# Q, k and v of a graph transformer layer by seven half-sized fp32 block products (Strassen's scheme), and the second group's rows transposed on TensorE

**Chip, cores, metric.** One core of one Trainium2 chip (trn2). The metric is the device time of one execution in microseconds, the median of several.

## The reference, cut to what matters

128 batches of 128 rows of 512 numbers go through two layers. The change touches only the projections of the first.

```python
h = jnp.maximum(_layernorm(x, axis=-1), 0.0)
q, k, v = (proj(Wq, bq), proj(Wk, bk), proj(Wv, bv))     # each: 'bse,fe->bsf', 512 x 512
scores = jnp.einsum('bhqd,bhkd->bhqk', q, k) * SCALE     # 8 heads of 64
attn = jax.nn.softmax(scores * mask, axis=-1)            # mask = 2 * adj
x = x + jnp.einsum('bse,fe->bsf', ctx, Wo) + bo          # ctx = attn @ v
# ... a graph attention layer with one 512 x 512 matrix, softmax over rows, elu
```

## The kernel before

Batches come in groups of four (G = 4). One iteration of the main loop handles scores and context of batch t, the output projection of t - 1 and the second layer of t - 2, and projects a quarter of q and k of the next group, so that TensorE (PE) always has something to do. Everything is fp32. The parts concerned:

```python
def qk_unit(g, n):                        # one of 8 blocks of q, k for a group of 4 batches
    f, is_k = divmod(n, 2)
    ...
    pp = ps1.tile([P, G * S], F32, name="pp", tag="ps1")
    for c in range(C):                    # C = 4 chunks of 128 of the contraction
        nc.tensor.matmul(pp, w[:, c, f * P : (f + 1) * P],
                         hTs[g][:, c].rearrange("p b s -> p (b s)"),     # 512 columns
                         start=(c == 0), stop=(c == C - 1))
    return lambda: nc.scalar.activation(dst, pp, AF.Identity, bias=...)  # eviction
def values(b):                            # v of one batch, 4 matmuls of 512 columns
    pv = rows_matmul(hTs[g][:, :, i, :], wv_sb)
    nc.scalar.copy(vs[b], pv)
def spread0(b): ...                       # mean and 1/std of each row: SBUF -> DRAM
def fetch0(b): ...                        # ... and back, as rows broadcast over partitions
def hidden(b): ...                        # transposed x -> hidden rows, with them
# start (cut): group 0's rows are transposed on TensorE, group 1's go by the DRAM trip
for n in range(2 * C):
    b = G + n // 2
    evict = qk_unit(0, n)
    if n % 2 == 0:
        stats0(b); spread0(b); fetch0(b)
    else:
        load_x0(b + G)
    evict()
    if n > 2 and n % 2:
        hidden(b - 1)
hidden(2 * G - 1)
# main loop (cut), iteration t:
    scores(t); evict = qk_unit(g + 1, 2 * i)
    scores1(t - 2)                        # second layer: one transpose (pb), softmax follows
    evict(); normalise(t); softmax1(t - 2); output0(t - 1); values(t); gather1(t - 2)
    qk_unit(g + 1, 2 * i + 1)(); hidden(ahead)
    attn_T(t); output1(t - 2); context(t)
```

Of the kernel before, what the change touches and what calls it, by code (L numbers as in the profile page):

```python
# [13 lines left out]
P = 128  # L14
# [3 lines left out]
H = 8  # L18
# [5 lines left out]
def kernel(  # L24
# [30 lines left out]
    work = ctx.enter_context(tc.tile_pool(name="work", bufs=2))  # L55
    small = ctx.enter_context(tc.tile_pool(name="small", bufs=6))
    ps1 = ctx.enter_context(tc.tile_pool(name="ps1", bufs=4, space=bass.MemoryType.PSUM))
    ps2 = ctx.enter_context(tc.tile_pool(name="ps2", bufs=2, space=bass.MemoryType.PSUM))

    xs, x0s, adjs, adjTs, hTs = {}, {}, {}, {}, {}  # L60
# [11 lines left out]
    def hT_slot(b):  # L72
        g, i = divmod(b, G)
        if i == 0:
            hTs[g] = grp.tile([P, C, G, S], F32, name="hT", bufs=3)
        return hTs[g][:, :, i, :]

    def load_xT(b):
        nc.sync.dma_start(hT_slot(b), xT[b])  # L79
# [30 lines left out]

    bq_sb = column(bq, "bq")
    bk_sb = column(bk, "bk")
    bv_sb = column(bv, "bv")
    wq_sb = weight(wqT, "wq")
    wk_sb = weight(wkT, "wk")
    for b in range(G, 2 * G):
        load_xT(b)
    wv_sb = weight(wvT, "wv")
# [6 lines left out]
    for b in range(2):  # L125
        load_adj(b)
# [24 lines left out]
    def norm0(b):  # L151
        mv, rstd = st0.pop(b)
        hns[b] = work.tile([P, E], F32, name="hn", tag="h2", bufs=4)
        nc.vector.tensor_scalar(hns[b], x0s.pop(b), mv[:, 0:1], rstd, op0=OP.subtract, op1=OP.mult)
# [18 lines left out]
    def fetch0(b):  # L173
        r = rows0[b]
        rows0[b] = small.tile([P, 2, S], F32, name="mr", bufs=3)
        nc.sync.dma_start(rows0[b].rearrange("p s k -> p (s k)"), r.rearrange("s p -> (s p)").partition_broadcast(P))

    def hidden(b):

        mr = rows0.pop(b)  # L180
        g, i = divmod(b, G)
        h = hTs[g][:, :, i, :]
# [10 lines left out]
    def qk_unit(g, n):  # L193

        f, is_k = divmod(n, 2)
        if n == 0:
            qks[g] = grp.tile([P, C, G * S], F32, name="qT"), grp.tile([P, C, G * S], F32, name="kT")
        w = wk_sb if is_k else wq_sb
        dst = qks[g][is_k][:, f]
        pp = ps1.tile([P, G * S], F32, name="pp", tag="ps1")  # L200
        for c in range(C):
            nc.tensor.matmul(  # L202
                pp, w[:, c, f * P : (f + 1) * P], hTs[g][:, c].rearrange("p b s -> p (b s)"),
                start=(c == 0), stop=(c == C - 1),
            )
        if is_k:
            return lambda: nc.scalar.activation(dst, pp, AF.Identity, bias=bk_sb[:, f : f + 1])  # L207
        return lambda: nc.scalar.activation(dst, pp, AF.Identity, bias=bq_sb[:, f : f + 1], scale=QSCALE)

    def values(b):  # L210
        g, i = divmod(b, G)
        pv = rows_matmul(hTs[g][:, :, i, :], wv_sb)
        vs[b] = work.tile([P, E], F32, name="v")
        nc.scalar.copy(vs[b], pv)  # L214

    def scores(b):
        g, i = divmod(b, G)
        qT, kT = qks[g]
# [7 lines left out]
        at = work.tile([P, H, S], F32, name="at", bufs=3)  # L226
        nc.vector.tensor_tensor(at, sc, adjs[b][:, None, :].to_broadcast([P, H, S]), OP.mult)  # L227
        nmx = small.tile([P, H], F32, name="nmx")
        nc.vector.tensor_reduce(nmx, at, AX.X, OP.max, negate=True)  # L229
        sums = small.tile([P, H], F32, name="sums")  # L230
# [19 lines left out]
    def context(b):  # L250

        pc = ps1.tile([P, C, S], F32, name="pc", tag="ps1")
        for i in range(C):
            for s in range(2):
                head = 2 * i + s
                nc.tensor.matmul(  # L256
                    pc[s * D : (s + 1) * D, i, :], vs[b][:, head * D : (head + 1) * D], ats[b][:, s * C + i, :],
# [5 lines left out]
    def output0(b):  # L263
        po = rows_matmul(cxs[b], wo_sb)
        nc.vector.tensor_tensor(xs[b], po, xs[b], OP.add)
        mv, rstd = row_stats(xs[b])

        h2 = work.tile([P, E], F32, name="h2", bufs=4)
# [24 lines left out]
    def softmax1(b):  # L293
        h2, w, nmx, rstd = l1s[b]
        sums = small.tile([P, 1], F32, name="sums1")
        nc.scalar.activation(w, w, AF.Exp, bias=nmx, accum_out=sums)
        rs = small.tile([P, 1], F32, name="rs1")
# [51 lines left out]


    with tc.manual_schedule():
        nc.scalar.mul(bq_sb, bq_sb, QSCALE)
        for b in range(G):
            stats0(b)
        for b in range(G):
            norm0(b)
            hidden_T(b)
            load_x0(G + b)
        for n in range(2 * C):
            b = G + n // 2  # L360
            evict = qk_unit(0, n)
            if n % 2 == 0:
                stats0(b)
                spread0(b)
                fetch0(b)
            else:
                load_x0(b + G)
            evict()
            if n > 2 and n % 2:
                hidden(b - 1)  # L370
        hidden(2 * G - 1)
        load_x(0)
        load_x(1)
        load_xT(2 * G)
        stats0(2 * G)
        spread0(2 * G)
        stats0(2 * G + 1)
        for t in range(B + 3):
            g, i = divmod(t, G)
            more = (g + 1) * G < B  # L380
            ahead = t + 2 * G
# [3 lines left out]
            if ahead < B:  # L385
                fetch0(ahead)
            if ahead + 4 < B:
                load_x0(ahead + 4)
            if ahead + 1 < B:
                spread0(ahead + 1)  # L390
            if t < B:
                scores(t)
            if more:
                evict = qk_unit(g + 1, 2 * i)
            if t == 1:
                spread_u()
            if 0 <= t - 2 < B:
                scores1(t - 2)
            if more:
                evict()  # L400
            if t < B:
                normalise(t)
            if 0 <= t - 2 < B:
                softmax1(t - 2)
            if 0 <= t - 1 < B:
                output0(t - 1)
            if t < B:
                values(t)
            if 0 <= t - 2 < B:
                gather1(t - 2)  # L410
            if more:
                qk_unit(g + 1, 2 * i + 1)()
            if ahead < B:
                hidden(ahead)
            if ahead + 2 < B:
# [50 lines left out]
```

## Time and profile before

| | before |
|---|---|
| median, lowest to highest of 3 | 2821.45 us, 2820.44 to 2821.62 |
| PE, VectorE (DVE), ScalarE (ACT) busy | 97%, 56%, 39% |
| steady iteration, scores to scores | 21.36 us, of it 10.31 us q, k and v |
| PE without work at the first iteration | 39.3 us |
| scores of batch 2 start | 122.65 us after the start |
| an iteration of the last group | 16.36 us |

How to read it: PE is the bound, so time is what PE does one thing after another. A matmul's busy time runs up to its modelled end, which overlaps the next one; the pace is read from the distance of starts. The prediction below shows the lines.

In the lines, `sc` is the scores, `pa` the transposes of the attention, `pc` the context, `pb` and `pg` the second layer's transpose and its gather. `pm` is a block with 512 columns: with `wo` the output projection, with `w` the second layer's matrix, with `wv` v. `pp` is q and k before the change; `acc_a` to `acc_c` are the products after it, one for each bank of PSUM, the memory that the matmuls write to and that ScalarE and VectorE read. `[39.3 <-DVE hT L184]` means that the engine had been idle for 39.3 us, and what released it. The granted clock is the share of TensorE's full clock that the profile shows as granted.

### The profile page before, as it was taken

How to read it: one execution, taken by the hardware profiler on the slowest of the kernel's cores; microseconds unless marked ns; L12 is line 12 of the kernel's file. 1: busy time of each engine (PE TensorE's matmuls, PEld its weight loads, DVE VectorE, ACT ScalarE, POOL GpSimd, SP SyncE). 2: the span in 40 equal slices, each digit the busy share in tenths (PEclk: the TensorE clock that was granted, in tenths of full speed). 3: DMA queues.
4: the chain of work that ended last, by engine and by line, in shares of the span. 5: the costliest groups of instructions: out<-in, count | busy, mean ns of one | idle time of the engine just before them, and what ended most of it. 6: DMA issues, size and time to landing. Idle time of an engine off the chain costs nothing.

```text
span 2821.7 us, 33182 instructions
## 1 busy us (share of the span) xinstructions
PE 2750.6 (97%) x11424; PEld 1431.5 (51%) x11424; DVE 1581.7 (56%) x3085; ACT 1100.9 (39%) x3336; POOL 415.2 (15%) x647
## 2 busy tenths in 40 slices
PE   4799999999999999999999999999999999999997
PEld 2355555555555555555555555555555555555554
DVE  1555655655555565565565555556556555555545
ACT  1334344334433433433433343343443334434343
POOL 1111111111111111111111111111111111111101
PEclk8999999999999999999999999999999999999999
DMA  5412112112212211211221221221121122122110
GB/s 151 58 61 71 57 57 74 57 57 70 62 57 63 69 57 56 75 57 56 71 61 57 65 67 57 59 73 56 57 72 60 56 67 65 57 61 60 34 38 19
DMA packets 214040, 174.55 MB, mean 62 GB/s; under 512 B 49648, under 2 KB 161776, under 8 KB 213872
## 3 DMA queue, kind: packets, MB, share of 16 engines
q1 hardware_dynamic: 212288, 172.42, 21.3%
q8 instruction: 91, 1.49, 0.4%
q14 instruction: 77, 0.63, 0.1%
q10 hardware_dynamic: 1584, 0.01, 0.0%
HBM read 138.68 MB, written 33.68 MB: 61 GB/s over the span
## 4 chain that ended last, share of the span: by engine, by line
PE 94%; DMA 3%; DVE 1%; ACT 1%; SPq 0%; issue 0%; POOL 0%; ACTq 0%; DVEq 0%
PE pm L142 46%; PE pp L202 31%; PE sc L225 5%; PE pc L256 5%; PE pg L307 4%; PE pa L245 4%; DMA rows<-mv 2%; ACT at L232 1%; PE pb L285 0%; DMA mr<-rows 0%; DMA c<-in_bo 0%; DVE nmx L229 0%; DVE at L227 0%; DVE junk L337 0%; DMA x<-in_x 0%; SPq L79 0%
## 5 line engine op out<-in xcount | busy, mean ns | idle before, releaser
L232 ACT ACTIVATE at<-at,nmx 128x128 f32<-128x128 f32 x1024 | 395.8, 388 | 426.9 <-DVE nmx L229 426.9
L202 PE MATMUL pp<-hT,wq 128*128 128x512 f32 x1024 | 474.9, 606 | 40.0 <-DVE hT L184 39.3
L135 POOL TENSOR_SCALAR mv<-mv 128x1 f32<-128x1 f32 x256 | 135.8, 530 | 2303.4 <-DVE mv L132 2303.2
L142 PE MATMUL pm<-w,gT 128*128 128x512 f32 x1024 | 463.1, 595 | 1.5 <-ACT gT L309 1.5
L142 PE MATMUL pm<-wv,hT 128*128 128x512 f32 x1024 | 460.4, 592 | 2.9 <-ACT u_src L347 2.9
L142 PE MATMUL pm<-wo,cxT 128*128 128x512 f32 x1024 | 460.8, 593 | 0.5 <-ACT cxT L261 0.5
L202 PE MATMUL pp<-hT,wk 128*128 128x512 f32 x1024 | 460.6, 592 | 0.0
L317 DVE SCALAR_TENSOR_TENSOR x<-pm,x 128x512 f32<-128x512 f32 x128 | 88.5, 691 | 641.9 <-ACT ez L316 641.9
L142 PEld LDWEIGHTS pm<-wv,hT 128*128 128x128 f32 x1024 | 194.5, 190 | 248.2 <-issue 244.4
L202 PEld LDWEIGHTS pp<-hT,wq 128*128 128x128 f32 x1024 | 184.9, 190 | 241.4 <-issue 186.0
L142 PEld LDWEIGHTS pm<-wo,cxT 128*128 128x128 f32 x1024 | 184.8, 190 | 220.0 <-issue 219.3
L288 DVE TENSOR_TENSOR w<-w,neg 128x128 f32<-128x128 f32 x128 | 37.4, 292 | 441.5 <-ACT w L287 441.5
L142 PEld LDWEIGHTS pm<-w,gT 128*128 128x128 f32 x1024 | 185.3, 191 | 187.1 <-issue 184.7
L202 PEld LDWEIGHTS pp<-hT,wk 128*128 128x128 f32 x1024 | 185.2, 190 | 186.5 <-issue 186.5
L214 ACT COPY v<-pm 128x512 f32<-128x512 f32 x128 | 74.9, 585 | 434.4 <-PE pm L142 434.3
L207 ACT ACTIVATE kT<-pp,bk 128x512 f32<-128x512 f32 x128 | 88.1, 688 | 357.6 <-PE pp L202 357.6
L136 POOL TENSOR_TENSOR mv<-mv,mhalf 128x1 f32<-128x1 f32 x256 | 200.0, 781 | 21.4
L316 ACT ACTIVATE ez<-pm 128x512 f32<-128x512 f32 x128 | 76.5, 598 | 316.2 <-PE pm L142 316.2
L130 DVE BATCH_NORM_STATS2 st<-x 128x6 f32<-128x512 f32 x256 | 176.7, 690 | 25.8 <-DMA x<-in_x 21.2
L232 ACT ACTIVATION_READ_ACCUMULATOR at<-at,nmx 128x1 f32 x1024 | 191.1, 187 | 0.0
L307 PEld LDWEIGHTS pg<-w,h 128*128 128x128 f32 x1024 | 134.8, 193 | 73.0 <-issue 68.7
L227 DVE TENSOR_TENSOR at<-sc,adj 128x1024 f32<-128x1024 f32 x128 | 156.7, 1224 | 6.1 <-PE sc L225 3.7
(59 smaller groups left out, 2763.7 us busy)
## 6 DMA issues: line engine op xcount, KB each, us to landing
x<-in_x SPq DMA_DIRECT2D x256, 256.0 KB, 3.8
out<-x SPq DMA_DIRECT2D x128, 256.0 KB, 2.1
hT<-in_xT SPq DMA_DIRECT2D x124, 256.0 KB, 3.3
mr<-rows SPq DMA_DIRECT2D x124, 128.0 KB, 3.6
adj<-in_adj SPq DMA_DIRECT2D x128, 64.0 KB, 2.8
adjT<-in_adjT SPq DMA_DIRECT2D x128, 64.0 KB, 3.0
rows<-mv SPq DMA_DIRECT2D x124, 1.0 KB, 9.3
wq<-in_wqT SPq DMA_DIRECT2D x1, 1024.0 KB, 7.1
```

The source lines that it names most:

```text
L130: nc.vector.bn_stats(st, src)
L135: nc.gpsimd.tensor_scalar_add(rstd, rstd, EPS)
L136: nc.gpsimd.tensor_tensor(rstd, rstd, mhalf, OP.pow)
L142: nc.tensor.matmul(pm, lhsT[:, c, :], w[:, c, :], start=(c == 0), stop=(c == C - 1))
L202: nc.tensor.matmul(pp, w[:, c, f * P : (f + 1) * P], hTs[g][:, c].rearrange("p b s -> p (b s)"), start=(c == 0), stop=(c == C - 1),)
L225: nc.tensor.matmul(sc[:, s * C + i, :], qT[r, i, cols], kT[r, i, cols], start=True, stop=True)
L227: nc.vector.tensor_tensor(at, sc, adjs[b][:, None, :].to_broadcast([P, H, S]), OP.mult)
L232: nc.scalar.activation(at[:, j, :], at[:, j, :], AF.Exp, bias=nmx[:, j : j + 1], accum_out=sums[:, j : j + 1])
L245: nc.tensor.transpose(pa[:, j, :], at[:, j, :], ident)
L256: nc.tensor.matmul(pc[s * D : (s + 1) * D, i, :], vs[b][:, head * D : (head + 1) * D], ats[b][:, s * C + i, :], start=True, stop=True,)
L307: nc.tensor.matmul(pg[:, c, :], h2[:, c * P : (c + 1) * P], w, start=True, stop=True)
L317: nc.vector.scalar_tensor_tensor(xs[b], pw, 0.0, xs[b], op0=OP.max, op1=OP.add)
```

## The change

The intent is to do less arithmetic on the engine that is the bound. The hidden rows of a group (512 x 512) and each weight (512 x 512) are cut into quarters of 256; q, k and v are each had from seven products of quarters instead of eight, at the price of sums: of weight quarters once, of hidden quarters once a group, and of products when they leave PSUM. Three PSUM banks (a, b, c) collect the products; "a" goes on accumulating after its value so far was read. The second part concerns the start: the second group's rows are normalised and transposed on TensorE, like the first's, instead of by the round trip of their statistics through DRAM.

The diff, cut to its core (`# ...` marks cuts, the other comments are added here):

```diff
-    ps1 = ctx.enter_context(tc.tile_pool(name="ps1", bufs=4, space=bass.MemoryType.PSUM))
-    ps2 = ctx.enter_context(tc.tile_pool(name="ps2", bufs=2, space=bass.MemoryType.PSUM))
+    ps1 = ctx.enter_context(tc.tile_pool(name="ps1", bufs=6, space=bass.MemoryType.PSUM))
+    ps2 = ctx.enter_context(tc.tile_pool(name="ps2", bufs=1, space=bass.MemoryType.PSUM))
# ... work pool bufs 2 -> 1, hT a tile of 7 quarters, weights loaded as quarters
+    def weight_sums(w):                       # once for each of q, k, v
+        nc.vector.tensor_tensor(w[:, 4], w[:, 1], w[:, 0], OP.subtract)
+        nc.vector.tensor_tensor(w[:, 5], w[:, 3], w[:, 4], OP.subtract)
+        nc.vector.tensor_tensor(w[:, 1], w[:, 3], w[:, 1], OP.subtract)
+        nc.vector.tensor_tensor(w[:, 6], w[:, 2], w[:, 5], OP.subtract)
+    PRODUCTS = [(0, 0, "a"), (1, 2, "b"), (5, 5, "a"), (6, 1, "c"), (4, 4, "a"), (2, 3, "a"), (3, 6, "c")]
+    def hidden_sums(g):                       # once a group
+        h = hTs[g]
+        nc.vector.tensor_tensor(h[:, 4], h[:, 2], h[:, 3], OP.add)
+        nc.vector.tensor_tensor(h[:, 5], h[:, 4], h[:, 0], OP.subtract)
+        nc.vector.tensor_tensor(h[:, 6], h[:, 0], h[:, 2], OP.subtract)
+        nc.vector.tensor_tensor(h[:, 2], h[:, 1], h[:, 5], OP.subtract)
-    def qk_unit(g, n):
# ...
+    def product(g, which, n):
+        ha, wb, bank = PRODUCTS[n]
# ...
+        for m in range(2):
+            ms = slice(m * P, (m + 1) * P)
+            for c in range(2):
+                lhsT, rhs = (h[:, c, ms], w[:, wb, c, :]) if which == "v" else (w[:, wb, c, ms], h[:, c, :])
+                nc.tensor.matmul(                                   # 256 columns
+                    acc[:, m, :], lhsT, rhs, start=fresh and m == 0 and c == 0, stop=c == 1, skip_group_check=True
+                )
# ... first(): ScalarE copies bank a out; add(): VectorE adds bank b or c to what is there
+    SEQ = ["q0", "q1", "q2", "q3", "q4", "k0", "q5", "k1", "q6", "k2", "k3", "k4", "v0", "k5", "v1", "k6"]
+    SEQ += ["v2", "v3", "v4", "v5", "v6"]
+    TICKS = [SEQ[0:5], SEQ[5:10], SEQ[10:15], SEQ[15:21]]
     with tc.manual_schedule():
# ... start: all 21 products of group 0, between them for each batch of group 1:
-                spread0(b)
-                fetch0(b)
+                    norm0(b)
+            if b < 2 * G and step == 3:
+                hidden_T(b)
+        stats0(2 * G)
# ... spread0(2 * G), stats0(2 * G + 1)
+        hidden_sums(1)
+        stats0(2 * G + 2)
# ... main loop:
+            if 0 <= t - 2 < B:
+                scores1(t - 2)                # now ahead of scores(t)
+                softmax1(t - 2)
             if t < B:
                 scores(t)
+                mask(t)                       # with the scale of q in it
+            done = unit(0)
# ... exps, hidden or hidden_sums, normalise, output0(t - 1), products 1 to 3
#     around hidden1 and gather1, attn_T(t), product 4, output1, product 5, context(t)
```

More of the change, by code (lines that the diff above doesn't have):

```diff
@@ L54 @@
     grp = ctx.enter_context(tc.tile_pool(name="grp", bufs=2))
-    work = ctx.enter_context(tc.tile_pool(name="work", bufs=2))
+    work = ctx.enter_context(tc.tile_pool(name="work", bufs=1))
     small = ctx.enter_context(tc.tile_pool(name="small", bufs=6))
-    ps1 = ctx.enter_context(tc.tile_pool(name="ps1", bufs=4, space=bass.MemoryType.PSUM))
-    ps2 = ctx.enter_context(tc.tile_pool(name="ps2", bufs=2, space=bass.MemoryType.PSUM))
-    xs, x0s, adjs, adjTs, hTs = {}, {}, {}, {}, {}
+    ps1 = ctx.enter_context(tc.tile_pool(name="ps1", bufs=6, space=bass.MemoryType.PSUM))
+    ps2 = ctx.enter_context(tc.tile_pool(name="ps2", bufs=1, space=bass.MemoryType.PSUM))
+    xs, x0s, adjs, adjTs, hTs, hslots = {}, {}, {}, {}, {}, {}
     def load_x(b):
@@ L74, in hT_slot @@
         if i == 0:
-            hTs[g] = grp.tile([P, C, G, S], F32, name="hT", bufs=3)
-        return hTs[g][:, :, i, :]
+            hTs[g] = grp.tile([P, 7, 2, 2 * S], F32, name="hT")
+        half, w = divmod(i, 2)
+        return hTs[g][:, 2 * half : 2 * half + 2].rearrange("p q c k -> p (q c) k")[:, :, w * S : (w + 1) * S]
     def load_xT(b):
-        nc.sync.dma_start(hT_slot(b), xT[b])
+        hslots[b] = hT_slot(b)
+        nc.sync.dma_start(hslots[b], xT[b])
     def load_adj(b):
@@ L109, in row, with quarters @@
         return b
+    def quarters(src, name):
+        w = const.tile([P, 7, 2, E // 2], F32, name=name)
+        nc.sync.dma_start(w[:, 0:4], src)
+        return w
     bq_sb = column(bq, "bq")
@@ L113 @@
     bv_sb = column(bv, "bv")
-    wq_sb = weight(wqT, "wq")
-    wk_sb = weight(wkT, "wk")
+    wq_sb = quarters(wqT, "wq")
+    wk_sb = quarters(wkT, "wk")
     for b in range(G, 2 * G):
-        load_xT(b)
-    wv_sb = weight(wvT, "wv")
+        load_x0(b)
+    wv_sb = quarters(wvT, "wv")
+    for b in range(2):
+        load_adj(b)
+        load_x(b)
     wo_sb = weight(woT, "wo")
@@ L123 @@
     ut_sb = row(a1, E, "u_dst")
-    for b in range(2):
-        load_adj(b)
+    def weight_sums(w):
[3 more added lines that the diff above has]
+        nc.vector.tensor_tensor(w[:, 6], w[:, 2], w[:, 5], OP.subtract)
     def row_stats(src):
@@ L152, in norm0 @@
         mv, rstd = st0.pop(b)
-        hns[b] = work.tile([P, E], F32, name="hn", tag="h2", bufs=4)
+        hns[b] = work.tile([P, E], F32, name="hn", tag="h2", bufs=3)
         nc.vector.tensor_scalar(hns[b], x0s.pop(b), mv[:, 0:1], rstd, op0=OP.subtract, op1=OP.mult)
@@ L174, in fetch0 @@
         r = rows0[b]
-        rows0[b] = small.tile([P, 2, S], F32, name="mr", bufs=3)
+        rows0[b] = small.tile([P, 2, S], F32, name="mr", bufs=4)
         nc.sync.dma_start(rows0[b].rearrange("p s k -> p (s k)"), r.rearrange("s p -> (s p)").partition_broadcast(P))
@@ L180, in hidden @@
         mr = rows0.pop(b)
-        g, i = divmod(b, G)
-        h = hTs[g][:, :, i, :]
+        h = hslots.pop(b)
         nc.vector.tensor_tensor(h, h, mr[:, 0:1, :].to_broadcast([P, C, S]), OP.subtract)
@@ L191, in shift @@
         nc.vector.tensor_tensor(xs[b], xs[b], c_sb, OP.add)
-    def qk_unit(g, n):
-        f, is_k = divmod(n, 2)
-        if n == 0:
-            qks[g] = grp.tile([P, C, G * S], F32, name="qT"), grp.tile([P, C, G * S], F32, name="kT")
-        w = wk_sb if is_k else wq_sb
-        dst = qks[g][is_k][:, f]
-        pp = ps1.tile([P, G * S], F32, name="pp", tag="ps1")
-        for c in range(C):
-            nc.tensor.matmul(
-                pp, w[:, c, f * P : (f + 1) * P], hTs[g][:, c].rearrange("p b s -> p (b s)"),
-                start=(c == 0), stop=(c == C - 1),
-            )
-        if is_k:
-            return lambda: nc.scalar.activation(dst, pp, AF.Identity, bias=bk_sb[:, f : f + 1])
-        return lambda: nc.scalar.activation(dst, pp, AF.Identity, bias=bq_sb[:, f : f + 1], scale=QSCALE)
@@ L210, in values @@
-    def values(b):
-        g, i = divmod(b, G)
-        pv = rows_matmul(hTs[g][:, :, i, :], wv_sb)
-        vs[b] = work.tile([P, E], F32, name="v")
-        nc.scalar.copy(vs[b], pv)
+    PRODUCTS = [(0, 0, "a"), (1, 2, "b"), (5, 5, "a"), (6, 1, "c"), (4, 4, "a"), (2, 3, "a"), (3, 6, "c")]
[5 more added lines that the diff above has]
+        nc.vector.tensor_tensor(h[:, 2], h[:, 1], h[:, 5], OP.subtract)
@@ new lines, with dst, first, add @@
+    accs = {}
+    def product(g, which, n):
+        if n == 0:
+            if which == "v":
+                vs[g] = grp.tile([P, G, E], F32, name="v")
+            else:
+                qks[g, which] = grp.tile([P, C, G * S], F32, name=which + "T")
+        w = {"q": wq_sb, "k": wk_sb, "v": wv_sb}[which]
+        ha, wb, bank = PRODUCTS[n]
+        fresh = (which, bank) not in accs
+        if fresh:
+            accs[which, bank] = ps1.tile([P, 2, 2 * S], F32, name="acc_" + bank, tag="ps1")
+        acc = accs[which, bank]
+        h = hTs[g][:, ha]
+        for m in range(2):
[5 more added lines that the diff above has]
+                )
+        def dst(t, f):
+            if which == "v":
+                return vs[g][:, 2 * t : 2 * t + 2, f * 2 * P : (f + 1) * 2 * P]
+            return qks[g, which][:, 2 * f : 2 * f + 2, t * 2 * S : (t + 1) * 2 * S]
+        def first(t, f):
+            a = accs[which, "a"]
+            if which == "v":
+                nc.scalar.copy(dst(t, f), a)
+            else:
+                bias = bk_sb if which == "k" else bq_sb
+                for m in range(2):
+                    j = 2 * f + m
+                    nc.scalar.activation(dst(t, f)[:, m, :], a[:, m, :], AF.Identity, bias=bias[:, j : j + 1])
+        def add(t, f, bank):
+            d = dst(t, f)
+            nc.vector.tensor_tensor(d, accs[which, bank], d, OP.add)
+        def done():
+            if n == 0:
+                first(0, 0)
+            elif n == 1:
+                add(0, 0, "b")
+                del accs[which, "b"]
+            elif n == 2:
+                first(1, 0)
+            elif n == 4:
+                first(1, 1)
+                add(1, 1, "c")
+            elif n == 5:
+                first(0, 1)
+                del accs[which, "a"]
+            elif n == 6:
+                add(1, 0, "c")
+                del accs[which, "c"]
+        return done
@@ L216, in scores @@
     def scores(b):
         g, i = divmod(b, G)
-        qT, kT = qks[g]
+        qT, kT = qks[g, "q"], qks[g, "k"]
         cols = slice(i * S, (i + 1) * S)
@@ L225, in scores, with mask, exps @@
                 nc.tensor.matmul(sc[:, s * C + i, :], qT[r, i, cols], kT[r, i, cols], start=True, stop=True)
-        at = work.tile([P, H, S], F32, name="at", bufs=3)
-        nc.vector.tensor_tensor(at, sc, adjs[b][:, None, :].to_broadcast([P, H, S]), OP.mult)
+        at = work.tile([P, H, S], F32, name="at", bufs=2)
+        ats[b] = at, sc
+    def mask(b):
+        at, sc = ats[b]
+        nc.vector.scalar_tensor_tensor(
+            at, sc, QSCALE, adjs[b][:, None, :].to_broadcast([P, H, S]), op0=OP.mult, op1=OP.mult
+        )
         nmx = small.tile([P, H], F32, name="nmx")
         nc.vector.tensor_reduce(nmx, at, AX.X, OP.max, negate=True)
+        ats[b] = at, nmx
+    def exps(b):
+        at, nmx = ats[b]
         sums = small.tile([P, H], F32, name="sums")
@@ L256, in context @@
                 nc.tensor.matmul(
-                    pc[s * D : (s + 1) * D, i, :], vs[b][:, head * D : (head + 1) * D], ats[b][:, s * C + i, :],
+                    pc[s * D : (s + 1) * D, i, :], vs[b // G][:, b % G, head * D : (head + 1) * D], ats[b][:, s * C + i, :],
                     start=True, stop=True,
@@ L265, in output0, with hidden1 @@
         nc.vector.tensor_tensor(xs[b], po, xs[b], OP.add)
-        mv, rstd = row_stats(xs[b])
-        h2 = work.tile([P, E], F32, name="h2", bufs=4)
+        l1s[b] = row_stats(xs[b])
+    def hidden1(b):
+        mv, rstd = l1s[b]
+        h2 = work.tile([P, E], F32, name="h2", bufs=3)
         nc.vector.tensor_scalar(h2, xs[b], mv[:, 0:1], 0.0, op0=OP.subtract, op1=OP.max)
@@ L296, in softmax1, with scale1 @@
         nc.scalar.activation(w, w, AF.Exp, bias=nmx, accum_out=sums)
+        l1s[b] = h2, w, sums, rstd
+    def scale1(b):
+        h2, w, sums, rstd = l1s[b]
         rs = small.tile([P, 1], F32, name="rs1")
@@ L347, in spread_u @@
             nc.scalar.copy(u, pu.rearrange("p c k -> p (c k)"))
+    SEQ = ["q0", "q1", "q2", "q3", "q4", "k0", "q5", "k1", "q6", "k2", "k3", "k4", "v0", "k5", "v1", "k6"]
+    SEQ += ["v2", "v3", "v4", "v5", "v6"]
+    TICKS = [SEQ[0:5], SEQ[5:10], SEQ[10:15], SEQ[15:21]]
     with tc.manual_schedule():
-        nc.scalar.mul(bq_sb, bq_sb, QSCALE)
         for b in range(G):
@@ L357 @@
             hidden_T(b)
-            load_x0(G + b)
-        for n in range(2 * C):
-            b = G + n // 2
-            evict = qk_unit(0, n)
-            if n % 2 == 0:
-                stats0(b)
-                spread0(b)
-                fetch0(b)
-            else:
-                load_x0(b + G)
-            evict()
-            if n > 2 and n % 2:
-                hidden(b - 1)
-        hidden(2 * G - 1)
-        load_x(0)
-        load_x(1)
-        load_xT(2 * G)
+        weight_sums(wq_sb)
+        hidden_sums(0)
+        for n, u in enumerate(SEQ):
+            done = product(0, u[0], int(u[1]))
+            if n == 1:
+                weight_sums(wk_sb)
+            if n == 6:
+                weight_sums(wv_sb)
+            b, step = divmod(n, 4)
+            b += G
+            if b < 2 * G:
+                if step == 0:
+                    load_x0(b + G)
+                    stats0(b)
+                elif step == 1:
+                    norm0(b)
+            done()
+            if b < 2 * G and step == 3:
+                hidden_T(b)
         stats0(2 * G)
@@ L377 @@
         stats0(2 * G + 1)
+        hidden_sums(1)
+        stats0(2 * G + 2)
+        fetch0(2 * G)
+        spread0(2 * G + 1)
         for t in range(B + 3):
             g, i = divmod(t, G)
-            more = (g + 1) * G < B
-            ahead = t + 2 * G
+            units = TICKS[i] if (g + 1) * G < B else []
+            unit = lambda n: product(g + 1, units[n][0], int(units[n][1])) if n < len(units) else (lambda: None)
+            far = t + 2 * G
             if t + 2 < B:
@@ L384 @@
                 load_x(t + 2)
-            if ahead < B:
-                fetch0(ahead)
-            if ahead + 4 < B:
-                load_x0(ahead + 4)
-            if ahead + 1 < B:
-                spread0(ahead + 1)
+            if far + 1 < B:
+                fetch0(far + 1)
+            if far + 4 < B:
+                load_x0(far + 4)
+            if far + 2 < B:
+                spread0(far + 2)
+            if 0 <= t - 2 < B:
+                scores1(t - 2)
+                softmax1(t - 2)
             if t < B:
                 scores(t)
-            if more:
-                evict = qk_unit(g + 1, 2 * i)
+                mask(t)
+            done = unit(0)
             if t == 1:
@@ L397 @@
             if 0 <= t - 2 < B:
-                scores1(t - 2)
-            if more:
-                evict()
+                scale1(t - 2)
+            done()
+            if t < B:
+                exps(t)
+            if i == 0:
+                for b in range((g + 2) * G, min((g + 3) * G, B)):
+                    load_xT(b)
+            elif (g + 2) * G < B:
+                if i < 3:
+                    hidden((g + 2) * G + 2 * i - 2)
+                else:
+                    hidden_sums(g + 2)
             if t < B:
                 normalise(t)
-            if 0 <= t - 2 < B:
-                softmax1(t - 2)
             if 0 <= t - 1 < B:
                 output0(t - 1)
-            if t < B:
-                values(t)
+            unit(1)()
+            if 0 <= t - 1 < B:
+                hidden1(t - 1)
+            unit(2)()
             if 0 <= t - 2 < B:
                 gather1(t - 2)
-            if more:
-                qk_unit(g + 1, 2 * i + 1)()
-            if ahead < B:
-                hidden(ahead)
-            if ahead + 2 < B:
-                stats0(ahead + 2)
+            done = unit(3)
+            if 0 < i < 3 and (g + 2) * G < B:
+                hidden((g + 2) * G + 2 * i - 1)
+            done()
             if t < B:
                 attn_T(t)
+            unit(4)()
+            if far + 3 < B:
+                stats0(far + 3)
+            if t < B:
                 if t == 0:
@@ L424 @@
                 output1(t - 2)
+            unit(5)()
             if t < B:
                 context(t)
-            if ahead + 1 < B:
-                load_xT(ahead + 1)
 def kernel(
@@ L436, with quarters @@
     from concourse.bass_utils import run_bass_kernel_spmd
+    def quarters(w):
+        w = np.reshape(w, (2, w.shape[0] // (2 * P), P, 2, -1))
+        return np.reshape(np.transpose(w, (2, 0, 3, 1, 4)), (P, 4, w.shape[1], -1))
     given = {
@@ L443 @@
         "adjT": np.transpose(adj, (0, 2, 1)),
-        "wqT": np.transpose(L0_gnn_Wq),
+        "wqT": quarters(np.transpose(L0_gnn_Wq)),
         "bq": L0_gnn_bq,
-        "wkT": np.transpose(L0_gnn_Wk),
+        "wkT": quarters(np.transpose(L0_gnn_Wk)),
         "bk": L0_gnn_bk,
-        "wvT": np.transpose(L0_gnn_Wv),
+        "wvT": quarters(np.transpose(L0_gnn_Wv)),
         "bv": L0_gnn_bv,
```

## The prediction

> **What bounds the kernel now.** I read the page's busy shares first, then the slices, then the order in time of TensorE (PE) in one steady iteration, then what PE waited for.
>
> The busy shares (engine, busy us, share of the span, instructions):
>
> ```profile
> PE 2750.6 (97%) x11424; PEld 1431.5 (51%) x11424; DVE 1581.7 (56%) x3085; ACT 1100.9 (39%) x3336; POOL 415.2 (15%) x647
> PE   4799999999999999999999999999999999999997
> PEclk8999999999999999999999999999999999999999
> ```
>
> PE is the only engine near its limit, and at full clock. But "busy" counts each matmul up to its modelled end; what an instruction really takes is read from starts. The order in time of PE (start, length, what):
>
> ```profile
> 1003.07 0.27 PE L285 MATMUL pb<-ident,ws 128*128 128x128 f32 x1
> 1003.18 3.60 PE L142 MATMUL pm<-wo,cxT 128*128 128x512 f32 x8
> 1006.62 3.60 PE L142 MATMUL pm<-wv,hT 128*128 128x512 f32 x8
> 1010.05 1.05 PE L307 MATMUL pg<-w,h 128*128 128x128 f32 x8
> 1010.94 3.60 PE L202 MATMUL pp<-hT,wk 128*128 128x512 f32 x8
> 1014.38 1.04 PE L245 MATMUL pa<-ident,at 128*128 128x128 f32 x8
> 1015.25 3.60 PE L142 MATMUL pm<-w,gT 128*128 128x512 f32 x8
> 1018.78 1.09 PE L256 MATMUL pc<-aT,v 128*64 128x128 f32 x16
> 1019.81 1.16 PE L225 MATMUL sc<-kT,qT 64*128 64x128 f32 x16
> ```
>
> Each start follows the last one's work without a hole. Four fp32 matmuls of 512 columns are eight instructions and take 1006.62 - 1003.18 = 3.44 us, 0.429 us an instruction; eight instructions of 128 columns take 1010.94 - 1010.05 = 0.89 us, 0.111 us each. One iteration (a batch), from one scores group to the next (998.45 to 1019.81 us), takes 21.36 us. Q, k and v are 24 instructions of 512 columns in it, 10.31 us; the other 11.05 us are not touched.
>
> What PE waited for over the whole run (engine, line, whom; us, times, longest):
>
> ```profile
> PE pp L202 <- DVE hT L184: 39.3, 1, 39.3
> PE pg L307 <- DVE w L299: 10.4, 5, 3.8
> PE pt L162 <- DVE hn L154: 8.5, 1, 8.5
> ```
>
> One hole of 39.3 us, at the first iteration: the second group's projections wait for its hidden rows. Behind it are four serial round trips of row statistics through DRAM; their store shows in the chain that ended last:
>
> ```profile
> 28.77 8.38 DMA rows<-mv
> 38.06 10.65 DMA rows<-mv
> 49.63 11.41 DMA rows<-mv
> 61.96 12.28 DMA rows<-mv
> ```
>
> Scores of batch 0 start at 40.5 us, PE goes on at 81.1 us. The second line of the waits (10.4 us) is the last group, where no next group fills PE: its iterations last 16.36 us.
>
> **What the Trainium skill says.** "TensorE: Matmul & The Clock Gate", section Back-to-back issue gap: a warm matmul of N columns follows the last after N/2.4 + 2.5 ns, 262 cycles for 256 columns. "FP8 and Floating Point Precision", section TensorE Precision Notes: true fp32 takes four passes. The trace agrees with both together: it has two instructions per fp32 matmul, and with two passes in each, 512 columns make 2 x 512/2.4 + 2.5 = 429 ns (measured 429) and 128 make 109 (measured 111). The same section warns that the weight load can set the pace at small N; at 128 columns the trace shows at most 2 ns of that, so 256 should not meet it. "VectorE: DVE Perf Modes", section The TRN2 errata, gives (N+151)/0.96 ns for an fp32 add of two tensors, 691 ns at 512; the trace has 673 to 692. "ScalarE: Activation LUTs", section What ACT_TABLE_LOAD costs, gives 280 + 0.833 N ns for an activation with a pointer bias, 493 at 256; I take the trace's own 347 ns at 128 and 679 at 512, which put 256 near 460.
>
> **The change part by part.**
>
> *Products.* A group of four batches had 12 blocks of eight instructions, 96 x 429 ns = 41.2 us. Now each of q, k, v has seven products of four matmuls with 256 columns: 21 x 4 x 2 = 168 instructions. Interpolated between the two measured paces, 256 columns take 111 + (429 - 111)/3 = 217 ns. 168 x 217 = 36.5 us; saved 4.75 us a group, 1.19 us an iteration. So seven eighths of the arithmetic becomes 0.885 of the time. Steady iteration: 11.05 + 36.5/4 = 20.17 us.
>
> *Sums.* DVE gains four hidden sums and nine adds out of PSUM per group, 13 x 0.69 = 9.0 us, 2.2 us an iteration on top of 12.3 (the windows of a steady iteration): 14.6 of 20.2 us. ACT loses 12 evictions of 512 (8 x 0.68 + 4 x 0.585 = 7.8 us a group) and gets 16 halves at 0.46 and 4 copies, 9.7 us: plus 0.5 an iteration on 8.6. Neither becomes the bound if the order holds.
>
> *The order.* The critical loop inside an iteration is scores, mask, maximum, eight exps, normalise, transposes. From the end of context: VectorE first finishes the output adds and the second layer's two short ops (1.9 us), then mask and maximum 2.5, exps 3.1, reciprocal and normalise 1.5, handovers 0.3: transposes may start at 9.3 us. PE has in that stretch pb and scores 1.2, four products 4 x 1.74, output 3.43 and gather 0.89: 12.4 us. So 3 us of slack. Products that accumulate onto a bank just read by ScalarE have something between them in every case; the tightest is v's product 5, after product 4 with only the transposes (0.87 us) between and a copy of 0.58 plus handovers to wait for: perhaps 0.1 us a group.
>
> *The start.* The second group comes by 16 transposes (1.8 us of PE), the DRAM round trip and its 39.3 us hole go. But v of group 0 moves into the start: PE from 12.8 us does 36.5 + 1.8 us and small waits, so scores of batch 0 near 52 us instead of 40.5. Then VectorE is behind: the last v add, three statistics (2.6) and the hidden sums of group 1 (2.7) stand before the first mask, which I put at 58; normalise is done near 65, and PE stalls some 4.5 us. The one-off constants follow (six us of VectorE, before iteration 1's mask). I work iteration 2's start out at 91 us; before it was 122.65. Gain 32 us.
>
> *The end.* The last group loses its v blocks (3.43 us), but is bound by the loop above: 9.3 + 0.87 + 3.43 + 1.03 = 14.65 us instead of 16.36, four times: gain 7 us. The tail after (27.2 us) stays.
>
> *Sum.* 91 + 122 x 20.17 + 4 x 14.65 + 27.2 = 2638 us. Check on the kernel before: 122.65 + 122 x 21.36 + 4 x 16.4 + 27.2 = 2821. I add 8 us for handovers: **2646 us**, 6.2% less.
>
> **The rivals.**
>
> *A fixed cost per matmul eats it.* If busy time were the pace (1.05 and 3.60 us for eight), 256 columns would take some 238 ns, or the weight load (190 ns each on PEld) could start to show. For it: halving the columns doubles the weight loads per column. Against: 128 columns run at 111 ns, so loads overlap. With 238 ns: 168 x 21 ns x 31 groups = 109 us more, 2755 us, still faster by 2.4%.
>
> *Handovers and VectorE become the bound.* One ps2 slot instead of two, single-buffered work tiles, PSUM banks held over iterations, VectorE at 72% in strict order. For it: six users of the accumulator wait on ScalarE or VectorE. Against: the slack above, and six banks in ps1. If each of the 21 products lost 0.1 us: 31 x 21 x 0.1 = 65 us, 2711 us. If VectorE's order stalled PE by 1 us in each iteration, 2770, hardly any gain over 2%.
>
> *Only the start gains.* If the pace gain vanished (both of the above), the 39 us of start and end remain: 2782 us, within 2%.
>
> **Range and chances.** The pace at 256 columns lies between two measured ones on a line, so I trust it within 5 ns (26 us). Stalls can only add. Range 2618 to 2700. Faster by over 2% means below 2765: only rivals together get there. Faster 0.96, within 2% 0.035, slower 0.005.
>
> **What would show it.** Right: blocks of eight 256-column instructions starting 1.74 us apart; a group of four iterations every 80.7 us; 13,744 matmul instructions; no DRAM round trip of statistics ahead of the first iterations, iteration 2's scores near 91 us; VectorE near 1870 us busy, ScalarE near 1160. Wrong: a pace of 230 ns or more; PE waits on ScalarE or VectorE that recur 31 times or more; mask starting late each iteration because VectorE is still on the adds; transposes waiting for normalise in the middle of the run. Most likely to be wrong by size is the start, since its order of VectorE work is worked out by hand.

## The result, and the profile after

| | before | after |
|---|---|---|
| median of 4 runs | 2821.53 us | 2660.3 us (2657.71 to 2661.3) |
| ratio, 95% interval | | 0.9427 (0.9411 to 0.9444) |
| steady iteration (mean of four) | 21.36 us | 20.29 us |
| scores of batch 2 start | 122.65 us | 93.79 us |
| an iteration of the last group | 16.36 us | 14.4 us, one of them 16.1 |
| matmul instructions | 11,424 | 13,744 |

The changed kernel is 5.7% faster. The prediction said 2646, in a range of 2618 to 2700.

The changed kernel's page, busy shares and the two slices that answer to those of before:

```profile
PE 2615.8 (98%) x13744; PEld 1882.8 (71%) x13744; DVE 1830.3 (69%) x3509; ACT 1151.3 (43%) x3595; POOL 334.7 (13%) x647
PE   7999999999999999999999999999999999999996
PEclk9999999999999999999999999999999999999999
```

PE is still the bound, with more instructions in less time, and VectorE went from 56 to 69%. The weight loads (PEld) rose from 51 to 71% and still run beside the matmuls.

One iteration of the changed kernel, the order in time of PE (start, length, what):

```profile
1027.52 0.32 PE L363 MATMUL pb<-ident,ws 128*128 128x128 f32 x1
1027.77 1.16 PE L290 MATMUL sc<-kT,qT 64*128 64x128 f32 x16
1028.87 1.99 PE L238 MATMUL acc_a<-hT,wq 128*128 128x256 f32 x8
1030.70 3.60 PE L157 MATMUL pm<-wo,cxT 128*128 128x512 f32 x8
1034.13 1.89 PE L238 MATMUL acc_b<-hT,wq 128*128 128x256 f32 x8
1035.86 1.89 PE L238 MATMUL acc_a<-hT,wq 128*128 128x256 f32 x8
1037.58 1.05 PE L389 MATMUL pg<-w,h 128*128 128x128 f32 x8
...
1047.36 0.32 PE L363 MATMUL pb<-ident,ws 128*128 128x128 f32 x1
1047.61 1.16 PE L290 MATMUL sc<-kT,qT 64*128 64x128 f32 x16
```

No line has a wait. Sixteen 256-column instructions start over 1037.58 - 1034.13 = 3.45 us, 216 ns each. From one scores group to the next, 19.84 us with five products; the fourth iteration of each group, with six, has 21.63. Together 81.15 us, 80.7 predicted. The new thing is at the top: scores start 0.25 us after pb. VectorE is done with normalise (L314) 1040.20 - (1035.07 + 1.23) = 3.90 us before the transposes that need it start:

```profile
1035.07 1.23 DVE L314 TENSOR_TENSOR at<-at,rs 128x1024 f32<-128x1024 f32 x1
1040.20 1.04 PE L320 MATMUL pa<-ident,at 128*128 128x128 f32 x8
```

What PE waited for in the changed kernel (us, times, longest):

```profile
PE pa L320 <- DVE at L314: 18.3, 6, 4.8
PE pt L177 <- DVE hn L169: 8.7, 1, 8.7
PE pg L389 <- DVE w L381: 3.9, 1, 3.9
```

The 39.3 us are gone. The first line is six waits, two in the first iterations and four in the last group; none recurs in the middle. So time came out of three places: 122 iterations 1.07 us shorter each (130 us), 28.9 us at the start, and 6.8 us in the four iterations of the last group (65.8 before, 59.1 now). That is 166 us, the difference of the two profiled spans (2821.7 and 2655.8); the medians differ by 161. The blocks account for the iteration: 42 instructions of 0.216 us are 9.07 us where q, k and v took 10.31, so 1.24 less, of which pb's new place takes back 0.14 (run 7). The rest of the reordering in the diff gained nothing that shows on PE.

### The profile page after: what moved, and what is told of

It reads as the page before. It is cut to its first block, busy times and chain, and to the rows that moved or that the text cites. A ratio compares the mean times of both kernels' runs of the same rounds, so it can differ in the third digit from the quotient of the medians. Undisturbed runs are those within 1.5% of the kernel's fastest.

```text
span 2655.8 us, 38303 instructions
## 1 busy us (share of the span) xinstructions
PE 2615.8 (98%) x13744; PEld 1882.8 (71%) x13744; DVE 1830.3 (69%) x3509; ACT 1151.3 (43%) x3595; POOL 334.7 (13%) x647
## 3 DMA queue, kind: packets, MB, share of 16 engines
q8 instruction: 109, 1.79, 0.4%
## 4 chain that ended last, share of the span: by engine, by line
PE 97%; DVE 2%; ACT 1%; DMA 1%; issue 0%; SPq 0%; ACTq 0%; DVEq 0%
PE pm L157 33%; PE acc_a L238 25%; PE acc_c L238 13%; PE acc_b L238 6%; PE sc L290 5%; PE pc L331 5%; PE pa L320 4%; PE pg L389 4%; PE pb L363 1%; ACT at L307 1%; DMA hT<-in_xT 0%; DVE at L314 0%; DVE nmx L300 0%; DVE at L296 0%; PE pt L177 0%; DMA x<-in_x 0%
## 5 line engine op out<-in xcount | busy, mean ns | idle before, releaser
L238 PE MATMUL acc_a<-hT,wq 128*128 128x256 f32 x1024 | 246.7, 384 | 0.0
L238 PE MATMUL acc_a<-hT,wk 128*128 128x256 f32 x1024 | 245.3, 382 | 0.0
L238 PE MATMUL acc_a<-wv,hT 128*128 128x256 f32 x1024 | 244.2, 381 | 0.7 <-ACT v L250 0.7
L238 PEld LDWEIGHTS acc_a<-hT,wq 128*128 128x128 f32 x1024 | 190.7, 191 | 40.5 <-issue 14.8
L238 PEld LDWEIGHTS acc_a<-wv,hT 128*128 128x128 f32 x1024 | 189.4, 190 | 38.6 <-issue 14.8
L238 PEld LDWEIGHTS acc_a<-hT,wk 128*128 128x128 f32 x1024 | 187.2, 190 | 38.6 <-issue 14.8
L322 ACT COPY aT<-pa 128x1024 f32<-128x1024 f32 x128 | 129.6, 1012 | 147.4 <-PE pa L320 144.7
L331 PEld LDWEIGHTS pc<-aT,v 128*64 128x64 f32 x2048 | 109.2, 136 | 83.4 <-issue 83.4
L255 ACT ACTIVATE kT<-acc_a,bk 128x256 f32<-128x256 f32 x256 | 107.4, 471 | 134.0 <-PE acc_a L238 134.0
L314 DVE TENSOR_TENSOR at<-at,rs 128x1024 f32<-128x1024 f32 x128 | 156.8, 1225 | 4.4
```

The costliest lines, as they stand in the source:

```text
L238: nc.tensor.matmul(acc[:, m, :], lhsT, rhs, start=fresh and m == 0 and c == 0, stop=c == 1, skip_group_check=True)
L255: nc.scalar.activation(dst(t, f)[:, m, :], a[:, m, :], AF.Identity, bias=bias[:, j : j + 1])
L314: nc.vector.tensor_tensor(at, at, rs[:, :, None].to_broadcast([P, H, S]), OP.mult)
L322: nc.scalar.copy(aT, pa)
L331: nc.tensor.matmul(pc[s * D : (s + 1) * D, i, :], vs[b // G][:, b % G, head * D : (head + 1) * D], ats[b][:, s * C + i, :], start=True, st ...
```

## The experiments

Eight kernels, all with correct results; "before" had medians of 2823.1 and 2823.5 us on these chips. The diffs are shortened.

**1. The transposes alone.** Kernel before, start only:

```diff
     for b in range(G, 2 * G):
-        load_xT(b)
+        load_x0(b)
# ... in the loop over the first eight blocks:
-                stats0(b); spread0(b); fetch0(b)
+                load_x0(b + G); stats0(b); norm0(b)
-            if n > 2 and n % 2:
-                hidden(b - 1)
-        hidden(2 * G - 1)
+            if n % 2:
+                hidden_T(b)
```

> The kernel before, with one part of the change: the second group's rows are loaded row-wise, normalised and transposed on TensorE, no Strassen products. Theory (the two parts add up): the 39.3 us hole at the first iteration goes, 16 transposes (1.8 us) come, so 2821.5 - 37.5 = 2784 us, and iteration 2's scores start near 85 us instead of 122.65; the iteration stays 21.36 us. Rival (the hole hides other waits at the start, such as statistics or constants, that take its place): 2795 to 2815 us.

Measured: 2784.98 us, ratio 0.9862 (0.9847 to 0.9877). The hole has no successor; the largest waits left in its list are those of before:

```profile
PE pg L307 <- DVE w L299: 10.0, 5, 3.8
PE pt L162 <- DVE hn L154: 8.5, 1, 8.5
PE pm L142 <- ACT u_src L347: 2.9, 1, 2.9
```

Scores of batch 2 start at 84.07 us. The transposes alone are worth 38 us: less than 2%, but the interval is clear of 1.

**2. The products alone.** Changed kernel, its start by the round trip:

```diff
-        load_x0(b)
+        load_xT(b)
# ... in the loop over the 21 products of group 0:
                 if step == 0:
-                    load_x0(b + G)
-                    stats0(b)
+                    stats0(b); spread0(b); fetch0(b)
                 elif step == 1:
-                    norm0(b)
+                    load_x0(b + G)
-            if b < 2 * G and step == 3:
-                hidden_T(b)
+        for b in range(G, 2 * G):
+            hidden(b)
```

> The changed kernel with the other part alone: products as in the change, the second group's rows by the round trip of their statistics through DRAM as before. Theory: the steady iteration is that of the changed kernel (20.29 us on average), only the start is longer: the first mask comes near 87 us instead of 57.7, because the hidden rows of the last batch are there at 81 us and VectorE works in order; so 2660 + 29 = 2689 us. Rival (v in the start hides most of the round trip): 2660 to 2672 us.

Measured: 2687.04 us, ratio 0.9513 (0.9497 to 0.9529). 2689 was expected. PE's new waits at the start are these:

```profile
PE acc_a L238 <- DVE hT L214: 16.9, 1, 16.9
PE acc_c L238 <- DVE qT L259: 7.0, 1, 7.0
PE acc_a L238 <- DVE hT L198: 2.4, 1, 2.4
```

The first and the third are for the sums and hidden rows of the second group. The second is not: VectorE adds q late there, because it stood 12.31 us, until 27.99, waiting for rows whose statistics come first in its order. Together 26.3 us where the kernel before had 39.3; the seven products of v of group 0 (12.1 us) now lie in the start, beside the trip. Scores of batch 2 start at 122.22 us, as in the kernel before (122.65), so this run's gain is all in the iterations and the end. The parts do not quite add: 38 us and 136 us alone, 161 together. The transposes are worth some 25 us once the products are there (27 by the medians, 24 by the ratios).

**3. The same arithmetic in 256 columns.** Kernel before, q, k and v:

```diff
-        for c in range(C):
-            nc.tensor.matmul(pp, w[:, c, f * P : (f + 1) * P], hTs[g][:, c]..., start=(c == 0), ...)
+        for half in range(2):
+            cols = slice(half * 2 * S, (half + 1) * 2 * S)
+            for c in range(C):
+                nc.tensor.matmul(pp[:, cols], w[:, c, f * P : (f + 1) * P], hTs[g][:, c]...[:, cols],
+                                 start=(half == 0 and c == 0), ...)
# ... values() likewise
```

> The kernel before, every 512-column matmul of q, k and v written as two of 256 columns: the same arithmetic, twice the instructions and weight loads. Theory (an instruction costs 0.83 ns a column and 2 to 5 ns fixed, weight loads hidden): 192 x 216 ns against 96 x 429 ns a group is 0.3 us more, 32 groups: 2821.5 + 9 = 2830 us. Rival (a fixed cost per matmul or the weight load shows, 238 ns an instruction): 4.5 us more a group, 2965 us.

Measured: 2829.36 us, ratio 1.0022 (1.0007 to 1.0037). The order in time of PE shows v's 16 instructions of 256 columns between 8 of 512 and the gather:

```profile
1003.76 3.60 PE L142 MATMUL pm<-wo,cxT 128*128 128x512 f32 x8
1007.20 3.62 PE L218 MATMUL pv<-wv,hT 128*128 128x256 f32 x16
1010.65 1.06 PE L316 MATMUL pg<-w,h 128*128 128x128 f32 x8
```

3.44 us in eight, 3.45 us in sixteen; the iteration has 21.42 us instead of 21.36. Halving the columns costs next to nothing, and the rival of a fixed cost per matmul (2965 us) is out.

**4 and 5. VectorE loaded on purpose.** Changed kernel, with four or eight idle operations:

```diff
                 scores(t)
+                if units and t > 3:
+                    for _ in range(4):          # run 5: 8
+                        idle = work.tile([P, E], F32, name="junk", bufs=1)
+                        nc.vector.tensor_tensor(idle, c_sb, c_sb, OP.max)
                 mask(t)
```

> The changed kernel with four idle VectorE maxima (512 elements, 2.76 us) ahead of each mask in iterations 4 to 123; the result stays right. Theory (slack: normalise ends 3.9 us before TensorE reaches the transposes of the attention, and VectorE has 14.5 of 20.3 us on average): no TensorE wait recurs, 2660 to 2666 us, though VectorE goes to 85%. Rival (VectorE is already nearly the bound, each sum costs time): 120 x 2.76 = 330 us more, 2990 us, or half of that.

Measured with four: 2661.57 us, ratio 0.9427, that of the changed kernel itself. VectorE is busy 2145.9 us (81%, 85 expected), and PE's waits are those of the changed kernel (18.2, 8.7 and 3.9 us in its first three lines). 2.76 us of VectorE work in each of 120 iterations cost nothing.

> The changed kernel with eight idle VectorE maxima (5.5 us) ahead of each mask in iterations 4 to 123. Theory (3.9 us of slack): the transposes now wait some 1.6 us or more in every iteration, and in the iterations with most VectorE work (16.2 us) VectorE itself is full: 120 x 1.6 to 120 x 2.5 more, 2850 to 2960 us, with TensorE waiting for normalise each time. Rival (slack much larger than read): under 2700 us.

Measured with eight: 3084.18 us, ratio 1.0922 (1.0902 to 1.0942). There is an end to the slack, as expected, but I expected 2850 to 2960, and a single cause. PE's waits:

```profile
PE pa L320 <- DVE at L314: 98.6, 66, 4.8
PE acc_a L238 <- ACT kT L255: 65.8, 30, 2.2
PE acc_a L238 <- ACT v L250: 58.9, 31, 1.9
PE pg L389 <- DVE w L381: 35.1, 96, 3.9
```

The expected wait for normalise is there, 1.33 us in each of 60 iterations (the other six waits of this line are those at the start and the end). Two more came that the expectation did not have. The products "k5" and "v4" wait, 30 and 31 times, for ScalarE to copy their bank, and in ScalarE's program the eight exps of this iteration stand ahead of that copy. The trace shows it keep that order: product "k4", whose bank is to be copied, was done at 1048.39, but ScalarE stood idle for 7.57 us for the late maximum, began the exps at 1050.11, and copied k only at 1053.20:

```profile
1050.11 0.40 ACT L307 ACTIVATE at<-at,nmx 128x128 f32<-128x128 f32 x1 [7.57 <-DVE nmx L300]
...
1053.20 0.81 ACT L255 ACTIVATE kT<-acc_a,bk 128x256 f32<-128x256 f32 x2
```

Then PE pays twice, as its lines show, and the windows (time, busy and count of PE, PEld, DVE, ACT, POOL, then the granted clock):

```profile
1054.07 3.78 PE L238 MATMUL acc_a<-hT,wk 128*128 128x256 f32 x8 [2.19 <-ACT kT L255]
1057.64 1.91 PE L320 MATMUL pa<-ident,at 128*128 128x128 f32 x8
...
1054.00:1059.00 5.00, 4.93 (x15) 4.08 (x16) 4.86 (x12) 1.80 (x5) 0.89 (x3) 0.50 0.00 0
```

After the wait the granted clock is 0.50, and the block takes 3.78 us instead of 1.89. Over the whole run the clock was 0.948 against 0.997, and PE's busy time rose by 190 us on the same instructions; how much of this is the clock, and how much the ends of blocks that no next block overlaps before a wait, the runs do not separate. The four lines and 5.5 us for the exps are 264 us of waits, 23 of them at the start and the end as in the changed kernel, so 241 more. With the 190 that is 431 us, the difference of the profiled spans (3086.9 and 2655.8); the medians differ by 424. VectorE is busy for 80% of this run, no more than in run 4: it is the order of its work, not its share, that stalls PE.

**6. Control.** The changed kernel on the chip of run 5 and the next two.

> Control: the changed kernel unchanged, on the chip of the next three. 2657 to 2662 us.

Measured: 2662.19 us, ratio 0.943 (0.9417 to 0.9442), 0.2 us above the range expected. In its profile the 122 iterations take 2475.6 us, the same as in the profile above; the start and the end differ (below).

**7. Where the second layer's transpose stands.** Changed kernel:

```diff
-            if 0 <= t - 2 < B:
+            if 0 <= t - 2 < B and not units:
                 scores1(t - 2)
                 softmax1(t - 2)
             if t < B:
                 scores(t)
                 mask(t)
             done = unit(0)
+            if 0 <= t - 2 < B and units:
+                scores1(t - 2)
+                softmax1(t - 2)
```

> The changed kernel with one thing put back: the second layer's transpose of its scores (pb) again comes after a full-array matmul (the first product) instead of between context and scores. Theory for the term that the prediction missed (0.12 us an iteration): scores start 0.25 us after pb there, where pb took 0.11 us before, so the placement costs 0.14 us in each of 122 iterations; 17 us less, 2643 us, and the group of four takes 80.6 us. Rival (the 0.14 us is pb's own and follows it wherever it stands, or the later softmax of layer two delays exps and gather): 2655 us or more.

Measured: 2643.64 us, ratio to before 0.9362 (0.9349 to 0.9375); by medians 18.5 us less than the control. The order in time of PE:

```profile
1039.29 1.09 PE L331 MATMUL pc<-aT,v 128*64 128x128 f32 x16
1040.31 1.16 PE L290 MATMUL sc<-kT,qT 64*128 64x128 f32 x16
1041.40 1.99 PE L238 MATMUL acc_a<-hT,wk 128*128 128x256 f32 x8
1043.23 0.27 PE L363 MATMUL pb<-ident,ws 128*128 128x128 f32 x1
1043.34 3.60 PE L157 MATMUL pm<-wo,cxT 128*128 128x512 f32 x8
```

The next work starts 0.11 us after pb here, 0.25 us in the changed kernel, and nothing else got longer: from the scores at 1020.62 to these is 19.69 us against 19.84. So the 0.14 us belongs to the place between the 64-column context and the 64-row scores, not to the transpose. Why PE takes it there, these runs do not show. It is 17 of the 18.5 us; for the rest, PE waited 3.14 us at the transposes of iteration 1 in the control's profile and 0.30 here.

**8. That, and a shorter start.** In addition to run 7:

```diff
+            if n == 16:                         # before the last v products of group 0
+                stats0(2 * G); spread0(2 * G); stats0(2 * G + 1)
+                hidden_sums(1)
+                stats0(2 * G + 2); fetch0(2 * G); spread0(2 * G + 1)
# ... and away from behind them
```

> The version that the traces point to: pb after the first product as in the run before, and the statistics and hidden sums of the groups to come issued before the last v products, in VectorE's idle time at 42.7 to 48.3 us, so that the first mask does not wait for them. Theory: first mask near 53 instead of 57.7 us, the 4.8 us stall at the first transposes goes or is under 1 us: 2643 - 5 = 2638 us. Rival (v's sums are then late and push the same wait elsewhere): no better than with pb alone.

Measured: 2635.7 us, ratio 0.9333 (0.932 to 0.9345), the best version: 1% better than the change by medians. The first mask starts at 53.10 us (57.72 in the changed kernel), the first transposes at 60.55 after a wait of 0.40 (64.64 and 4.84 in run 7, from which this run differs in the start alone):

```profile
60.55 1.06 PE L320 MATMUL pa<-ident,at 128*128 128x128 f32 x8 [0.40 <-DVE at L314]
61.46 1.89 PE L238 MATMUL acc_a<-hT,wq 128*128 128x256 f32 x8
63.19 3.60 PE L409 MATMUL pm<-wo,bv 128*128 128x512 f32 x8
```

The gain by medians is 8 us, not 5. Run 7's lines at that place say why:

```profile
64.64 1.94 PE L320 MATMUL pa<-ident,at 128*128 128x128 f32 x8 [4.84 <-DVE at L314]
66.37 3.57 PE L238 MATMUL acc_a<-hT,wq 128*128 128x256 f32 x8
69.78 3.60 PE L409 MATMUL pm<-wo,bv 128*128 128x512 f32 x8
```

After its wait the two blocks took 69.78 - 64.64 = 5.14 us at a granted clock of 0.50, here 63.19 - 60.55 = 2.64 at 1.00: 2.50 us of slow clock. The wait of 0.30 us in iteration 1, where the hidden rows had waited for a transfer, went as well. With the 4.44 us of the wait itself that is 7.24 us; scores of batch 2 start at 85.81 us here and at 92.89 in run 7, 7.08 us earlier. (The two profiled spans differ by 5.9 only: here the clock fell after three of the last group's waits, in run 7 after two.)

## Why the prediction was right, by its own steps

| term | predicted | measured in the profiled run |
|---|---|---|
| scores of batch 2 start | 91 | 93.79 |
| 122 iterations | 122 x 20.17 = 2461 | 2569.39 - 93.79 = 2475.6, 20.29 each |
| four iterations of the last group | 4 x 14.65 = 58.6 | 59.1 |
| tail | 27.2 | 27.35 |
| handovers, added in one lump | 8 | (in the terms above) |
| sum | 2646 | 2655.8, as run 2657.7; median 2660.3 |

In the control's profile the start is 96.34, the 122 iterations 2475.6, the last group 60.75 and the tail 27.6: the iterations repeat, the start and the end vary from one execution to the next.

- **The pace** was right: 216 ns at 256 columns, 217 interpolated. Run 3 shows that it holds for plain matmuls too.
- **The iteration** was 0.12 us too short. The pace gives back 0.05 (42 instructions of about 1.2 ns less). The move of pb, which the prediction saw in the diff and gave no cost ("pb and scores 1.2"), costs 0.14, shown by run 7. The wait that the prediction put at 0.1 us a group, for v's product 5, shows as 0.06: that block's successor starts 1.79 us after it instead of 1.73. The 8 us for handovers was a guess of half the right size for a cause of another kind: 0.12 x 122 = 15 us. That it brought the sum nearer is luck.
- **The slack** was right as a mechanism, and on the safe side. Normalise ends 3.9 us before the transposes; predicted 3. Four idle operations were free, eight were not.
- **VectorE and ScalarE**: 1830 and 1151 us busy, 1870 and 1160 predicted. An eviction of one half of q or k took 470 ns, 460 interpolated.
- **The start**: the hole went as said, and VectorE's backlog stood before the first mask, at 57.7 us (58 predicted) with a wait of 4.84 us (4.5). The 2.8 us too much are about two things that were not in the sum: the clock after this wait (the two blocks took 69.24 - 65.05 = 4.19 us, 1.55 more than in run 8) and a second wait of 1.45 us in iteration 1. In the control the two are 2.51 and 3.14, and the start is 5.3 us too long. The prediction named the start as most likely to be wrong by size. Its sign "no DRAM round trip" holds for the second group only: the 120 batches after it still make it.
- **The end**: 14.4 us an iteration, three times; the other took 16.1, its output block running at a mean granted clock of 0.68 after one of the waits of 3.0 us. That the term came out right is luck, two errors that cancel; in the control two of the four iterations are long. A small misreading: of the 10.4 us that the prediction put down to the last group, one wait of 3.79 us lies in the tail.
- **The rivals**: a fixed cost per matmul is refuted (run 3). VectorE as the bound is refuted for the change (run 4), but its lateness stalls PE from somewhere between 2.8 and 5.5 us more (run 5). "Only the start gains" is refuted: the start alone gives 1.4% (run 1), the products alone 4.9% (run 2).

Open stays why pb costs more between two tiled stages, and where exactly between four and eight operations the slack ends.

## What to carry to other kernels

When one engine is the bound, read its pace from the distance of starts at two sizes and interpolate; the busy time of a block of eight, shared out, would have been wrong by a tenth here (238 against 216 ns). Seven products for eight pay (0.88 of the time for 0.875 of the arithmetic) if the half-sized instruction keeps its pace and another engine has room for the sums, and how much room there is can be tested by adding idle work to it. When moving code for scheduling, look at what each instruction now stands between on the bound engine: one 0.11 us transpose in the wrong place cost 0.14 us in every iteration, a tenth of what the whole change won.

## What the Trainium skill lacked or had wrong

- "TensorE: Matmul & The Clock Gate", Back-to-back issue gap, says that the isolated-gap formula over-counts at 512 columns in a real kernel (131 ns sustained against 216) and under-counts at 128 (81 against 56). Here a dense stream with a weight load for every matmul follows the formula at all three sizes, two passes an instruction: 429, 216 and 111 ns for 512, 256 and 128 columns against 429, 216 and 109.
- "FP8 and Floating Point Precision", TensorE Precision Notes, has four passes for fp32. It does not say that the trace shows two instructions, each as long as two passes and with a weight load of its own (168 instructions for 84 matmuls a group).
- "TensorE: Matmul & The Clock Gate", Part 1, gives a window of about 3.4 us of idleness for the clock's return to half. Less was enough here: in run 5 a wait of 2.19 us was followed by a granted clock of 0.50, and in the changed kernel one of four waits of 3.0 us was followed by a mean of 0.68 (an output block of 5.28 us instead of 3.60).
- "TensorEngine Tiling (Array Packing)", Key Properties, says that changing the tiling mode drains TensorE, but neither it nor another page has the time that this costs: a full-array transpose between a 64-column and a 64-row stage took 0.25 us to the next start, between two full-array blocks 0.11. That such a drain is the cause of the 0.14 us is not shown here.
